# A graph layer on one core: rows that TensorE multiplies, fetched by GpSimd, ScalarE and now SyncE

## The chip, the core and the metric

The kernel runs on one core of one Trainium2 chip. The time is device time in microseconds of one execution. Before the change the median of three runs is 15399.93 us (15397.0 to 15401.84). One further execution was recorded by the hardware profiler; it took 15395.35 us, and its span from the first to the last instruction is 15393.3 us.

The names of the engines: PE is TensorE (matmul), PEld its weight load, DVE is VectorE, ACT is ScalarE, POOL is GpSimd and SP is SyncE. ACT and SP also issue DMAs; an ending q (ACTq, SPq) marks such instructions of an engine's queue.

## The reference, cut to what matters

There are 50000 nodes with 160 numbers each (64 scalars and 32 vectors of 3) and 1650000 edges: 800000 random ones in both directions, and one from each node to itself. They are sorted by destination. For each edge the row `x[src]` is fetched, combined with the edge's four numbers `e` and small weight matrices, and summed at `dst`:

```python
ss, vv = (s[src], v[src])
dot = jnp.einsum('eui,ei->eu', vv, e1)
out0 = C0 * (ss * e0 @ W1 + dot * INV3 @ W2)
...
m_agg = jax.ops.segment_sum(m, dst, num_segments=n)
h = jnp.concatenate([hs, hv.reshape(n, 3 * MUL1)], axis=1)
return x + jax.nn.relu(h)
```

After that each node's row gets its layer norm. Since everything between the fetch and the sum is linear, the kernel first sums, for every destination, the source rows weighted with each of the edge's four numbers, and applies the weights once for each node.

## The kernel before, in words

**Units, tiles, sets.** 128 edges are a unit. A unit needs the 128 rows `x[src]`, 640 bytes each, one in each partition of a tile `xg`. Six units make a group and three groups a pair (`PG = 3`; 18 units; there are 696 pairs). The change's title calls a pair a tile. Seven pairs (21 groups, 126 units) make a set (`SG`), and the edges' own data (source, destination, four numbers) are loaded a set at a time.

**Fetching rows.** `gather` (L427) fetches a unit's rows with one indirect DMA on POOL (L433), which takes the 128 row numbers from a tile `sources`. The tile `xg` has four buffers of one pair each. POOL does almost nothing else.

**Rows that ACT fetches.** One unit in every 2.5 pairs isn't gathered by POOL. `ask_alone` (L402) lets ACT fetch its rows one by one: for each of the four groups of 32 rows a register load (TENSOR_LOAD, L416) reads 32 byte addresses from the tile `where`, and then 32 DMAs of 640 bytes follow (L421), each with a register move before it. They land in `alone_scalar`, which has three buffers. `address` (L394) makes `where` for a set on DVE (L398, L399). `ask_alone` is a generator that yields after every row; the main loop takes three rows after each unit (`ALONE["scalar"]` is `(2.5, 0, 3)`: a unit every 2.5 pairs, offset 0, three rows a step) and begins a unit `LEAD` = 4 pairs ahead of the pair that uses it. PE waits for the 128 landings on a semaphore just before the unit's matmul (in `group_sums`, L465).

**Multiplying.** For each unit `spread` (L438) makes on DVE the weight tile `ha` (L445): at which of 32 nearby destinations an edge lands, times its four numbers. It does so for a whole pair, `AHEAD` = 3 pairs before its use; `ha` has `AHEAD + 1` buffers. PE multiplies `ha` by the rows (L474) and sums a group's six units in PSUM. `turn_sums` (L484) transposes the sums of the last pair on DVE (L488) and adds them into a ring of node sums (L497).

**Work beside it.** Every 7.1 pairs four blocks of nodes are finished: SP loads their rows `xt` (L741), PE multiplies the ring by the weights (L812), DVE takes the norm (L815 to L900), with a square root on ACT (`do_root`, L894), and SP writes `out` (L906). As often, SP loads the rows of a new segment of 512 nodes, `xr` in four parts, with the numbers `sa` of their edges to themselves (`ask_own`, L773 and L776), five pairs ahead, and DVE begins the segment's part of the ring with them (`set_own`). SP also loads each set's edges (`load`, L275 and L269, at the beginning of the set before it), DVE turns them (`do_cast`, `place`), and `place` also gives `sources` to POOL. Last, the edges of nodes to themselves have to be taken out of the list, so that they take no unit: 16 packs do this on DVE for 128 stretches of 790 edges each; SP reads a pack's input (L571 to L575) and stores it row by row: a register load (L698), then 16 DMAs of 18.5 KB and 0.5 KB in turn (L715), 17 such steps in a pack.

**What sets the order.** SP, PE, DVE and ACT run their instructions in the order in which the code issues them; the main loop over pairs `p` and units `j` is that order. After each unit's matmul it issues some of the work beside it (`work`, with a queue of tasks that `hand_over` fills after a pair), then some rows of `ask_alone`, then a step of the current pack as its due time wants it. An instruction that waits holds all that stands behind it on its engine.

## Time and profile before

| what | value |
|---|---|
| median of three runs | 15399.93 us |
| the profiled execution's own time | 15395.35 us |
| its span | 15393.3 us |
| mean granted TensorE clock | 0.576 |
| gathers on POOL | 12249 |
| units fetched by ACT | 267 (34176 rows) |
| rows' DMAs on SP | none |

How to read it: the page gives busy time by engine, but register loads, moves, semaphore waits and the issuing of DMAs are not counted as busy. ACT is therefore shown as 1% busy though it issues DMAs most of the time, and SP isn't in the list at all. What ACT and SP do is read from the timeline of their queues, where consecutive instructions of one kind are merged into one row with their count. A matmul in float32 appears as two records, so a unit counts double on PE.

### The profile page before, as it was taken

What the parts mean: (1) busy time and instruction counts of PE and PEld (TensorE: products, weight loads), DVE (VectorE), ACT (ScalarE), POOL (GpSimd) and SP (SyncE); (2) the same over time, 40 slices, a digit from 0 to 9 for tenths busy, and PEclk for the clock granted to TensorE, in tenths of its full rate; (3) what the DMA queues carried; (4) which work ended last, traced back from release to release, by engine and by line L of the source; (5) the groups of instructions that cost most, each with busy time, mean ns of one, the idle gap of its engine ahead of it and who ended that gap; (6) DMA issues with size and microseconds to landing.
All of it is one profiled execution on the core that took longest, in us unless ns stands there. A gap on an engine that the chain in (4) does not pass through costs nothing.

```text
span 15393.3 us, 164322 instructions
## 1 busy us (share of the span) xinstructions
PE 10745.6 (70%) x28959; PEld 6884.0 (45%) x28960; DVE 6891.3 (45%) x9468; ACT 138.6 (1%) x172; POOL 11614.3 (75%) x12263
## 2 busy tenths in 40 slices
PE   6767767676667676666766776766767676667666
PEld 3444444444444444444444444444444444444444
DVE  5534535344353544535344453544535435354333
ACT  0000000000000000000000000000000000000000
POOL 7777777777777777777777777777777777777777
PEclk5555555555555555555556555555555555555555
DMA  3333333333333333333333333333333333333332
GB/s 99 81 99 80 86 93 82 97 83 89 90 85 91 86 87 90 86 92 83 96 84 85 95 80 98 80 88 90 84 95 82 90 90 84 92 85 85 84 83 71
DMA packets 778898, 1347.79 MB, mean 88 GB/s; under 512 B 277566, under 2 KB 536537, under 8 KB 761621
## 3 DMA queue, kind: packets, MB, share of 16 engines
q0 software_dynamic: 587952, 1004.22, 27.7%
q1 hardware_dynamic: 120272, 310.14, 7.3%
q10 hardware_dynamic: 69616, 22.89, 0.8%
q14 instruction: 828, 6.77, 0.2%
q8 instruction: 230, 3.77, 0.1%
HBM read 1264.17 MB, written 72.09 MB: 87 GB/s over the span
## 4 chain that ended last, share of the span: by engine, by line
POOL 60%; issue 23%; DMA 12%; PE 4%; DVE 1%; POOLq 0%
POOL xg L433 60%; DMA xg<-in_x,sources 12%; PE ps L474 3%; PE phb L812 0%; DVE ha L445 0%; DVE xt L815 0%; DVE st L817 0%; DVE xr L791 0%; DVE ring L497 0%; DVE prow L663 0%; DVE ring L795 0%; DVE pri L658 0%; DVE sums L488 0%; DVE mv L819 0%; DVE marks L656 0%
## 5 line engine op out<-in xcount | busy, mean ns | idle before, releaser
L433 POOL DMA_INDIRECT xg<-in_x,sources x12249 | 11609.0, 948 | 3753.2 <-issue 3539.1
L474 PE MATMUL ps<-xg,ha 128*128 128x160 f32 x24498 | 9834.9, 513 | 4624.8 <-DMA xg<-in_x,sources 4521.5
L474 PEld LDWEIGHTS ps<-xg,ha 128*128 128x128 f32 x24498 | 5780.7, 293 | 8482.6 <-DMA xg<-in_x,sources 8005.4
L488 DVE STREAM_TRANSPOSE sums<-ps 128x480 f32<-128x480 f32 x696 | 474.3, 681 | 6929.9 <-PE ps L474 6909.2
L445 DVE TENSOR_TENSOR ha<-hot,pk 128x2304 f32<-128x2304 f32 x696 | 1776.0, 2552 | 23.9
L812 PE MATMUL phb<-BWk,ring 128*128 128x160 f32 (+1 forms) x3910 | 1294.8, 421 | 6.0 <-issue 5.2
L812 PEld LDWEIGHTS phb<-BWk,ring 128*128 128x128 f32 (+1 forms) x3910 | 1104.5, 325 | 7.0 <-issue 5.5
L497 DVE TENSOR_TENSOR ring<-ring,sums 128x160 f32 x2086 | 684.6, 328 | 354.2 <-issue 206.8
L815 DVE SCALAR_TENSOR_TENSOR xt<-phb,xt 128x320 f32<-128x320 f32 x196 | 96.0, 490 | 970.7 <-PE phb L812 970.6
L442 DVE TENSOR_TENSOR hot<-bank,rel 128x576 f32<-128x576 f32 x696 | 521.0, 749 | 0.1
L663 DVE COPY_PREDICATED prow<-marks,prow 128x4734 f32<-128x4734 int32 (+6 forms) x80 | 432.7, 5409 | 0.6
L795 DVE STREAM_TRANSPOSE ring<-xr 128x2560 f32<-128x2560 f32 x96 | 429.3, 4472 | 3.3
L663 DVE COPY_PREDICATED pra<-marks,pra 128x3156 f32<-128x3156 int32 (+6 forms) x80 | 294.8, 3684 | 0.0
L791 DVE TENSOR_TENSOR xr<-xr,bank 128x2560 f32<-128x2560 f32 x96 | 270.1, 2814 | 9.4 <-DMA xr<-in_x 6.1
L474 PE MATMUL ps<-alone_scalar,ha 128*128 128x160 f32 x534 | 196.5, 471 | 0.0
L474 PEld LDWEIGHTS ps<-alone_scalar,ha 128*128 128x128 f32 x534 | 160.1, 335 | 0.0
L494 DVE TENSOR_TENSOR ring<-ring 128x199 f32<-128x199 f32 (+20 forms) x485 | 150.1, 375 | 2.3
L894 ACT ACTIVATE rstd<-mv,eps_t 128x4 f32<-128x4 f32 (+1 forms) x99 | 29.4, 297 | 13513.0 <-DVE mv L819 12291.4
L900 DVE TENSOR_SCALAR xt<-xt,mv,rstd 128x160 f32<-128x160 f32 x391 | 123.2, 376 | 3.6
L751 DVE MEMSET ring<- 128x1255 f32 (+2 forms) x97 | 109.8, 1131 | 20.1 <-issue 19.9
L817 DVE BATCH_NORM_STATS2 st<-xt 128x6 f32<-128x160 f32 x391 | 108.1, 318 | 6.7
L377 DVE STREAM_TRANSPOSE pk<-raw 128x512 f32<-128x512 f32 x100 | 104.2, 1042 | 2.5 <-DMA raw<-in_attr 2.5
(342 smaller groups left out, 1661.5 us busy)
## 6 DMA issues: line engine op xcount, KB each, us to landing
alone_scalar<-in_x ACTq DMA_DIRECT2D x34176, 0.6 KB
xg<-in_x,sources POOLq DMA_INDIRECT x12249
xr<-in_x SPq DMA_DIRECT2D x380, 320.0 KB
edges<-prow SPq DMA_DIRECT2D x2030, 18.5 KB
raw<-edges SPq DMA_DIRECT2D x97, 384.0 KB
selves<-mine SPq DMA_DIRECT2D x2028, 0.5 KB
xt<-in_x SPq DMA_DIRECT2D x97, 320.0 KB
out<-xt SPq DMA_DIRECT2D x97, 320.0 KB
```

Of the source, the lines that this page charges most:

```text
L433: tc.add_to_no_dep_group(f"gathered{s % 2}", nc.gpsimd.indirect_dma_start(out=xg[:, j, :], out_offset=None, in_=x, in_offset=bass.Indirect ...
L442: nc.vector.tensor_tensor(hot[:, :n], slotsP[:, 0:W].unsqueeze(1).to_broadcast([P, n, W]), rel[:, u:u + n].unsqueeze(2).to_broadcast([P, n ...
L445: nc.vector.tensor_tensor(ha[:, :n], hot[:, :n].unsqueeze(2).to_broadcast([P, n, NK, W]), pk[:, :, u:u + n].rearrange("p k u -> p u k").un ...
L474: mm = nc.tensor.matmul(ps[:, j // G, :], ha[:, j].rearrange("p k w -> p (k w)"), xr, start=j % G == 0, stop=j % G == G - 1)
L488: nc.vector.transpose(at[:, :ng], ps[:, :ng].rearrange("p g (b f) -> p g b f", f=FB))
L494: nc.vector.tensor_tensor(ring[k][:, b, :past], ring[k][:, b, :past], ring[k - 1][:, b, S:S + past], op=ALU.add)
L497: nc.vector.tensor_tensor(here, here, at[:, i], op=ALU.add)
L663: nc.vector.copy_predicated(what[:n, a:e], mi[:, r].unsqueeze(2).to_broadcast([n, e - a, what.shape[2]]), what[:n, a + d:e + d])
L791: nc.vector.tensor_tensor(xr[:, :nq], xr[:, :nq], sumP[:, :nq].unsqueeze(2).to_broadcast([P, nq, D]), op=ALU.mult)
L795: nc.vector.transpose(ring[k][:, :, c0:c0 + nq * W].rearrange("p b (w q) -> p q b w", q=nq), xr[:, :nq].rearrange("p q (b f) -> p q b f", ...
L812: wrote("misc", nc.tensor.matmul(ph[:nb, h - h0], nodes, BWk[:, i, :], start=i == 0, stop=i == ND - 1))
L900: nc.vector.tensor_scalar(xt[:n, h], xt[:n, h], mv[:n, h, 0:1], rstd[:n, h:h + 1], op0=ALU.subtract, op1=ALU.mult)
```

## The change

SP fetches units too. `ALONE` gets `"sync": (3.0, 1, 3)`: one unit in 3 pairs, that is in 54 units, from pair 22 on; it is the last unit of its pair, and ACT's is now the one before the last. The rows of both are dealt evenly: after each unit a share of 1.03 x 128 / (every x 18) rows is added for each engine (2.44 for SP, 2.93 for ACT) and that many whole rows are issued, in place of three. Each engine has its own three buffers.

The other numbers go with it. A unit is begun 6 pairs ahead in place of 4 (`LEAD`), the segment's own rows are asked 7 pairs ahead in place of 5 (`OWN`), a set's edges are loaded in the fifth pair of the set two before it, which is 10 pairs ahead of its first use in place of 7 (`EARLY`), and `address` is issued in the second pair of a set in place of the third. The packs are due two or three pairs earlier, to match. `AHEAD` goes from 3 to 2, so `ha` has three buffers in place of four, and `place` is issued two pairs ahead of the next set.

```diff
-AHEAD = 3
+AHEAD = 2
-ALONE = {"scalar": (2.5, 0, 3)}
-LEAD = 4
+ALONE = {"sync": (3.0, 1, 3), "scalar": (2.5, 0, 3)}
+LEAD = 6
+OWN = 7
+EARLY = 4
...
+        alonep = {name: later_pools.enter_context(tc.tile_pool(name=f"alone_{name}", bufs=ALONE[name][2])) for name in ALONE}
...
         def do_cast(s):
             raws[s] = cast(raws[s])
-            address(*raws[s])
...
-            due.append(min((first - 1) * per - 1, first_of[own] // PG - 5))
+            due.append(min((first - 2) * per + EARLY - 1, first_of[own] // PG - OWN))
...
-                after_pair(p - 5, ask_own, k, bs, got)
+                after_pair(p - OWN, ask_own, k, bs, got)
...
-            if p % per == 0 and s + 1 < NSC:
-                end = reach(s + 1)
+            early = 1 if p == 0 else s + 2 if p % per == EARLY else NSC
+            if early < NSC:
+                end = reach(early)
...
-                raws[s + 1] = load(s + 1)
+                raws[early] = load(early)
+            if p % per == 1 and s + 1 < NSC and (s + 1) * SG >= NH:
+                address(*[raws[s + 1][i] for i in (0, 1, 5)])
...
-                    for _ in range(ALONE[name][2]):
-                        if name in asking and next(asking[name], 0) == 0:
+                    if name in asking:
+                        share[name] += 1.03 * P / (ALONE[name][0] * PG * G)
+                    while name in asking and share[name] >= 1:
+                        share[name] -= 1
+                        if next(asking[name], 0) == 0:
                             del asking[name]
```

On POOL the program changes in the number of gathers of a set. These rows are the start of its program before; the two `sources` tiles belong to alternate sets, and a full set is 126 gathers.

```order
L536 IOTA at 16x128
L433 DMA xg<-in_x,sources_136 128x160 x71
L433 DMA xg<-in_x,sources_137 128x160 x126
L433 DMA xg<-in_x,sources_136 128x160 x126
L433 DMA xg<-in_x,sources_137 128x160 x123
```

The same rows now:

```order
L538 IOTA at 16x128
L435 DMA xg<-in_x,sources_139 128x160 x78
L435 DMA xg<-in_x,sources_140 128x160 x126
L435 DMA xg<-in_x,sources_139 128x160 x126
L435 DMA xg<-in_x,sources_140 128x160 x121
```

From the fourth set on a set has 120 or 121 gathers in place of 123 or 124. Over the whole program the count goes from 12249 to 12029; ACT fetches 266 units in place of 267, and SP 221.

On SP these rows stand in the fourth set before, where the first units fetched row by row are asked for (`sa` and `xr` are a segment's own rows, `fd` and `raw` a set's edges):

```order
L773 DMA sa<-selves 128x1x64
L776 DMA xr<-in_x 32x2560 x4
L906 DMA out<-xt 128x640
L275 DMA fd<-edges 128x1x1
L269 DMA raw<-edges 128x2x384
L741 DMA xt<-in_x 128x640
```

And now, from the first row that SP asks for:

```order
L908 DMA out<-xt 128x640
L743 DMA xt<-in_x 128x640
L418 TENSOR_LOAD where
L423 DMA alone_sync<-in_x 1x640 x32
L418 TENSOR_LOAD where
L423 DMA alone_sync<-in_x 1x640 x11
L775 DMA sa<-selves 128x1x64
L778 DMA xr<-in_x 32x2560
L423 DMA alone_sync<-in_x 1x640 x10
L778 DMA xr<-in_x 32x2560
```

What stood together on SP now has rows between it, and a load that waits holds rows behind it. In all, SP issues 28288 rows and 884 register loads more.

More of the change, by code (lines that the diff above doesn't have):

```diff
@@ L240, in tile_gnn_resnorm @@
             tc.tile_pool(name="psM", bufs=1, space=PSUM) as psM, ExitStack() as later_pools:
-        wherep, alonep = (later_pools.enter_context(tc.tile_pool(name=name, bufs=bufs))
-                          for name, bufs in (("where", 2), ("alone", 3)))
+        wherep = later_pools.enter_context(tc.tile_pool(name="where", bufs=2))
+        alonep = {name: later_pools.enter_context(tc.tile_pool(name=f"alone_{name}", bufs=ALONE[name][2])) for name in ALONE}
         spotp, ownp = (later_pools.enter_context(tc.tile_pool(name=name, bufs=bufs))
@@ L392, in tile_gnn_resnorm, with address @@
         kept = {name: [tc.alloc_semaphore(f"own_{name}{i}") for i in range(SEMS)] for name in ALONE}
-        def address(s, at, fd, ef, af):
+        def address(s, at, ef):
             where = wherep.tile([P, NK, W], I32, name="where")
@@ L408, in ask_alone @@
             eng, kind = {"sync": (nc.sync, ET.SP), "scalar": (nc.scalar, ET.Activation)}[name]
-            to = alonep.tile([P, D], F32, name=f"alone_{name}")
+            to = alonep[name].tile([P, D], F32, name=f"alone_{name}")
             sem, uses = kept[name][asked[name] % SEMS], asked[name] // SEMS + 1
@@ L996, in tile_gnn_resnorm @@
         to_ask = {name: deque(range_of(every, at)) for name, (every, at, _) in ALONE.items()}
-        asking = {}
+        asking, share = {}, {name: 0.0 for name in ALONE}
         turning = None
         for p, (s, g, ng) in enumerate(pairs):
-            if p % per == 0 and s + 1 < NSC:
-                end = reach(s + 1)
+            early = 1 if p == 0 else s + 2 if p % per == EARLY else NSC
+            if early < NSC:
+                end = reach(early)
                 assert end <= 0 or rows_stored[0] == NR or end <= row_start(rows_stored[0])[0][0]
-                raws[s + 1] = load(s + 1)
-                if s + 2 == NSC:
-                    after_pair(p + 4, examine_all)
-                    after_pair(p + 6, read_flags)
+                raws[early] = load(early)
+            if p % per == 1 and s + 1 < NSC and (s + 1) * SG >= NH:
+                address(*[raws[s + 1][i] for i in (0, 1, 5)])
+            if p % per == 0 and s + 2 == NSC:
+                after_pair(p + 4, examine_all)
+                after_pair(p + 6, read_flags)
             if p % per == 2 and s + 1 < NSC:
```

## The prediction

> **What bounds the kernel now.** The page comes first: the engines, the groups, the chain that ended last.

> ```profile
> span 15393.3 us, 164322 instructions
> PE 10745.6 (70%) x28959; PEld 6884.0 (45%) x28960; DVE 6891.3 (45%) x9468; ACT 138.6 (1%) x172; POOL 11614.3 (75%) x12263
> POOL 60%; issue 23%; DMA 12%; PE 4%; DVE 1%; POOLq 0%
> L433 POOL DMA_INDIRECT xg<-in_x,sources x12249 | 11609.0, 948 | 3753.2 <-issue 3539.1
> L663 DVE COPY_PREDICATED prow<-marks,prow 128x4734 f32<-128x4734 int32 (+6 forms) x80 | 432.7, 5409 | 0.6
> q0 software_dynamic: 587952, 1004.22, 27.7%
> q10 hardware_dynamic: 69616, 22.89, 0.8%
> ```

> POOL's gathers are 60% of the chain, and most of the rest is "issue", the time before a gather in which it waits for nothing visible. POOL's 75% busy is thus a full engine: 948 ns of work and some 0.3 us of pause for each of 12249 gathers. The waits of POOL and three rows of its timeline (first, tenth from the last, last) confirm it.

> ```profile
> POOL xg L433 <- issue: 3539.1, 11606, 0.4
> POOL xg L433 <- PE ps L474: 154.9, 508, 0.3
> POOL xg L433 <- DMA xg<-in_x,sources: 50.8, 108, 1.8
> 6.13 1.13 POOL L433 DMA_INDIRECT xg<-in_x,sources  x1 [0.43 <-DVE center L330]
> 15354.61 0.95 POOL L433 DMA_INDIRECT xg<-in_x,sources  x1 [0.30 <-issue]
> 15367.11 0.95 POOL L433 DMA_INDIRECT xg<-in_x,sources  x1 [0.30 <-DMA xg<-in_x,sources]
> ```

> No wait for another engine is above 0.3 us, the usual pause. The last ten gathers come every 1.250 us; over all, (15367.11 - 6.13) / 12248 = 1.254 us. So a gather that is not issued is worth 1.25 us, as long as nothing else comes too late.

> ACT is the second engine to look at, since it does today what SP is to do.

> ```profile
> L421 ACTq DMA_DIRECT2D alone_scalar<-in_x x34176: 227/228/1754, 388.0 to 15100.3; - x200
> L416 ACTq TENSOR_LOAD <-where x1068: 2140/2298/4294, 385.7 to 15087.6; - x178
> 7047.19 0.30 ACT L894 ACTIVATE rstd<-mv,eps_t 128x4 f32<-128x4 f32 x1 [151.94 <-DVE mv L819]
> 7047.25 148.16 ACTq L421 DMA_DIRECT2D alone_scalar<-in_x  x364
> 7201.05 0.30 ACT L894 ACTIVATE rstd<-mv,eps_t 128x4 f32<-128x4 f32 x1 [153.56 <-DVE mv L819]
> 7355.20 150.11 ACTq L421 DMA_DIRECT2D alone_scalar<-in_x  x363
> 7509.75 145.70 ACTq L421 DMA_DIRECT2D alone_scalar<-in_x  x351
> ```

> Register loads included, a row costs ACT 148.16 / 364 = 0.407 us, a unit 52.1 us; a unit is wanted every 14712.3 / 267 = 55.1 us. In the cycle shown ACT ends its rows at 7195.41 and waits 5.6 us for DVE before the square root: it is nearly full, and not late.

> SP's own work today is one such cycle of loads (about 7 pairs), and the stores of the packs: a register load and 16 DMAs a step, 17 steps. The last rows are first and last store of a step, then the last store of that pack.

> ```profile
> 7223.61 0.36 SPq L906 DMA_DIRECT2D out<-xt  x1
> 7224.02 0.43 SPq L741 DMA_DIRECT2D xt<-in_x  x1
> 7224.49 0.58 SPq L275 DMA_DIRECT2D fd<-edges  x1
> 7225.12 0.61 SPq L269 DMA_DIRECT2D raw<-edges  x1
> 7246.43 0.54 SPq L773 DMA_DIRECT2D sa<-selves  x1
> 7253.80 1.73 SPq L776 DMA_DIRECT2D xr<-in_x  x4
> L698 SPq TENSOR_LOAD <-spots x272: 1157/1252/1925, 91.1 to 14280.1; - x136
> 7375.02 0.32 SPq L715 DMA_DIRECT2D edges<-prow  x1
> 7381.05 0.23 SPq L715 DMA_DIRECT2D selves<-mine  x1
> 7615.91 0.23 SPq L715 DMA_DIRECT2D selves<-mine  x1
> SPq L715 <- DMA edges<-prow: 365.3, 778, 3.2
> SPq L715 <- DMA selves<-mine: 208.5, 611, 1.8
> SPq L906 <- DVE xt L900: 9020.1, 95, 127.7
> ```

> A cycle's loads are 4.25 us. A step is 1.25 + 6.26 us and two gaps, 7.6 us; the waits for earlier stores, (365.3 + 208.5) / 272 = 2.1 us, bring it to 9.7 at most. I take 8.0. A pack's stores spread over 241 us. SP's long wait at L906 is idle time that rows can use.

> **The change, part by part.**

> *Gathers removed.* 220 x 1.250 to 1.254 = 275.0 to 275.9 us; I take 275.5, all of it on the path. A pair now has 18 - 1/2.5 - 1/3 = 17.27 gathers, 21.65 us in place of 17.6 x 1.254 = 22.07.

> *Rows on SP: do they fit?* They are asked from pair 16 on, and the last unit is used in pair 682: of 15125 us, 16 and 13 pairs of 18 x 1.254 us fall away, and 14470 remain. No trace shows rows on SP, so ACT's are the nearest. Lower bound: 0.407 us a row, 52.1 a unit. Upper: two sequencers issuing at once may slow each other. While SP stored a pack, ACT's rows took 150.11 / 363 = 0.4135 and 145.70 / 351 = 0.4151 us, 7 to 8 ns more, at 272 / 241 = 1.13 SP DMAs a microsecond. (One register load more or less in such a stretch is 2.3 / 360 us, 6 ns a row, so this is known to a factor of two at best.) ACT will issue 128 / 54.1 = 2.37, 2.1 times as many, so by proportion 14 to 17 ns: 0.421 to 0.424. It can't well be below nothing, since neither sequencer does anything for the other. I take 0.421, 53.9 us a unit, because the loaded stage is the nearer row. Then 221 x 53.9 = 11912, 15 packs (the first is stored before) x 17 x 8.0 = 2040, and 95 cycles x 4.25 = 404: 14356 of 14470 us, 99.2%. With the lower bounds (52.1 and 7.6) it is 95.8%, with the upper ones (54.3 and 9.7) 102.8%.

> Of the register loads the rows say 2.30 us for 32 values and 1.25 for 16. [...]

> *ACT, in less time.* A unit is now wanted every 2.5 x 21.65 = 54.1 us. SP will issue 128 / 65.0 = 1.97 rows a microsecond, 1.74 times the rate of the loaded stage, plus its stores a quarter of the time: 14 ns on average, 0.421 us a row, 53.9 a unit; 266 units and 94 square roots at 0.30 are 14365 us of 14490. It fits by 1%.

> *Leads.* A unit's rows are dealt over 128 / 2.44 = 52 units, 2.9 pairs, so they are asked 4.0 pairs, 87 us, before use. Landing takes what a gather's takes:

> ```profile
> 7004.40 2.57 DMA xg<-in_x,sources
> ```

> That leaves 84 us. In a store stage SP has 17 x 8.0 + 241 x 53.9 / 65.0 + 241 x 4.25 / 152 = 343 us of work in 241, so it ends 102 late; off the stages it has 14% spare and wins back about 100 in the 700 us to the next. PE would then wait some 18 us for rows at a stage's end. Four `xg` buffers let POOL run three pairs, 65 us, ahead of a late PE; `place` gives it new `sources` 2.8 pairs, 61 us, ahead. So POOL first waits where SP is 145 us late. Own rows (4 pairs after the last part's request), sets of edges (4 pairs to `address`) and `xt` (3.5 pairs, 76 us) stand behind the same rows on SP: DVE may wait some 25 us for `xt`, and POOL still doesn't. For ACT the same margin is 4.5 pairs less the landing, 94 us, and 60 more: some 150 us in all.

> *At nothing.* `ha` two pairs ahead in place of three: 43 us cover DVE's longest instruction, 5.4 us (L663); without the cover PE waits, not POOL, up to those 61 us. `address` one pair earlier moves half a microsecond on DVE; it can make SP and ACT wait for `where` only where DVE is late for a set's edges, and these are now asked 3 pairs sooner. PE gets 221 more semaphore waits, hidden by its 30% of idle time. The DMA engines get 28288 rows, 0.7% more by q10's 0.8% for ACT's.

> Sum: the profiled 15395.35 lies 4.6 us under the median of 15399.93 and the removed work is the same in both, so the median becomes 15399.9 - 275.5 = 15124.4; rounded, 15125.

> **The rivals.**

> *Slower: two row streams slow each other.* Place: each row's issue on ACT and SP. If they share one path, a row could cost far more than 14 ns extra, since the store stage had only 1.13 DMAs a microsecond against it, in bursts. ACT uses up its 14490 us, its 150 us of margin and the whole gain at 14915, that is at 0.437 us a row, 30 ns above 0.407; that is the point. At 35 ns its work is 266 x 128 x 0.442 + 28 = 15077 us, and the time 15125 + (15077 - 14640) = 15560. For it: both sequencers are at 99%, with no room for error. Against: twice the extra measured in the loaded stage would still be gone only in part. Chance 0.10.

> *Store stages spill over.* Steps at 9.7 us and rows at 0.424 make 102.8%, 404 us too much; less the 145 us that SP may be late before POOL waits, up to 260 is lost: 15385. A middle case, 102%, is 289 too much, loses 144 and comes to about 15270. For it: the lag of 102 us is won back only just. Against: the waits of 2.1 us come where stores follow one another, and rows now lie between steps. Chance 0.18, of it 0.05 so near the end that the time is within 0.2%.

> *The gathers' pace is not POOL's.* If the 16 DMA engines set the 1.25 us, rows moved to another queue take the same engines' time and nothing is won: 15400. Against it, gathers under different traffic (the first column behind the window is its length, then busy time and count, clock, DMA share, GB/s):

> ```profile
> 400.00:2000.00 1600.00, 1210.25 (x1279) 0.57 0.36 87
> 15150.00:15390.00 240.00, 165.03 (x175) 0.58 0.30 70
> ```

> 946 and 943 ns, at 0.36 and 0.30 of the DMA engines, of which gathers have 27.7%: the price follows POOL's work. Chance 0.02. [...]

> That the change doesn't do what it says is excluded by the program's rows: 12029 gathers, 221 units on SP.

> **How the numbers follow.** The forecast, 15125, has 0.70. Faster by over 0.2% (30 us, about what a measurement of this kernel can tell from no change) are the forecast and the spill up to 15369: 0.70 + 0.13 = 0.83. Within 0.2%: 0.05 + 0.02 = 0.07. Slower: 0.10. The forecast's own range is 15095 (all that the mean pace has over 1.250 us is won as well, 12029 x 0.004 = 48, of which I allow 30) to 15200. The whole range goes on to the spill's end, 15390; what lies above is the first rival and half of the cases without change, some 0.13, and little lies below.

> **What would show it.** Right: some 12029 gathers still every 1.25 us; no POOL wait for PE above the 0.3 us pause; ACT's and SP's rows at 0.42 us; PE waiting up to 20 us at the ends of store stages. Wrong: rows at 0.43 us or more on either; POOL waiting microseconds for PE or DVE; ACT never again waiting for DVE before a square root; gathers slower than 948 ns.

## The result and the profile after

| | before | changed kernel |
|---|---|---|
| median | 15400.88 us (15397.0 to 15401.84, 4 runs) | 16068.88 us (16059.6 to 16097.72, 4 runs) |
| ratio to before, 95% interval | | 1.0438 [1.0421, 1.0454] |
| profiled execution, span | 15393.3 us | 16057.9 us |
| gathers on POOL | 12249 | 12029 |

Faster was forecast, and the kernel is 4.4% slower. These are the page's lines of the changed kernel: the span, the queues, the chain and two groups.

```profile
span 16057.9 us, 221715 instructions
q0 software_dynamic: 577392, 986.19, 27.8%
q1 hardware_dynamic: 176848, 328.36, 7.4%
q10 hardware_dynamic: 69360, 22.81, 0.9%
PE 0%; DMA 0%; DVE 0%; POOL 0%; issue 0%
L435 POOL DMA_INDIRECT xg<-in_x,sources x12029 | 11398.8, 948 | 4627.2 <-issue 3150.1
L476 PE MATMUL ps<-alone_sync,ha 128*128 128x160 f32 x442 | 171.2, 490 | 1002.2 <-PEq L475 1002.2
```

The chain is of no use here: its shares are all 0%. The group of the gathers says more. There are 220 fewer and each still takes 948 ns, but POOL's idle time before them has risen from 3753.2 to 4627.2 us. A second group is new: PE waits 1002.2 us at L475 for rows that SP fetched. Two stories offer themselves, and POOL's waits in the changed kernel tell which of them holds POOL (total us, times, longest us):

```profile
POOL xg L435 <- issue: 3150.1, 10119, 3.6
POOL xg L435 <- DMA xg<-in_x,sources: 1390.5, 1708, 3.6
POOL xg L435 <- PE ps L476: 72.9, 180, 4.2
```

For PE it waits hardly at all (72.9 us, of which 180 x 0.3 are the usual pauses). What has grown is a gather's wait for another gather's landing, from 50.8 us in 108 waits to 1390.5 in 1708. Taken from the start times of all gathers, what each comes later than 1.251 us after the one before adds up to 53 us in the kernel before and to 990 us here. That is the result: 990 - 53 = 937, less the 275.5 saved, is 662 us, and the span has grown by 664.6.

The loss isn't spread evenly. Three stretches of the changed kernel (length, POOL's busy time and gathers, clock, DMA share, GB/s), of which the middle one is a store stage of SP:

```profile
7175.00:7550.00 375.00, 237.90 (x252) 0.56 0.35 76
7650.00:8050.00 400.00, 300.71 (x317) 0.58 0.36 86
8150.00:8340.00 190.00, 119.00 (x127) 0.57 0.35 76
```

In the store stage, where SP has both rows and stores to issue, a gather comes every 400 / 317 = 1.26 us, as before. Off the stages, where SP has time for its rows, one comes only every 190 / 127 = 1.50 us. So POOL stands where SP is early, not where it is late. The DMA engines' share is the same 0.35 to 0.36 in all three, no higher than the 0.36 of the kernel before. These are POOL's waits in the store stage and then in the last stretch:

```profile
POOL xg L435 <- issue: 96.9, 307, 3.6
POOL xg L435 <- DMA xg<-in_x,sources: 1.2, 4, 0.3
```

```profile
POOL xg L435 <- DMA xg<-in_x,sources: 48.6, 58, 1.8
POOL xg L435 <- issue: 22.1, 67, 1.9
```

And this is POOL gather by gather in that stretch (start, length, the pause before it and what ended it):

```profile
8201.49 0.94 POOL L435 DMA_INDIRECT xg<-in_x,sources  x1 [1.75 <-DMA xg<-in_x,sources]
8202.97 0.94 POOL L435 DMA_INDIRECT xg<-in_x,sources  x1 [0.54 <-DMA xg<-in_x,sources]
8204.98 0.94 POOL L435 DMA_INDIRECT xg<-in_x,sources  x1 [1.07 <-DMA xg<-in_x,sources]
8206.23 0.95 POOL L435 DMA_INDIRECT xg<-in_x,sources  x1 [0.30 <-issue]
```

Which gather's landing is it? Each gather's record names its semaphore. There are eight, 142 to 149, used in turn, and each gather adds to its own in sixteen steps. So a gather has to wait until the one eight before it has landed, and eight are issued in 8 x 1.25 = 10 us. Put beside each other from the trace (us from the span's start):

```
gather    pause   eight before:  issued   15th step  16th step
8201.49    1.75                 8188.25    8190.81    8201.23
8202.97    0.54                 8189.56    8192.25    8202.71
8204.98    1.07                 8190.81    8194.76    8204.72
8206.23    0.30                 8192.06    8194.94    8205.54
```

Each of the three held gathers starts 0.26 us after the sixteenth step of the gather eight before. Of 1254 pauses above 0.5 us in the whole trace, 1081 end within 0.5 us of that step. And it is only the sixteenth that is late: in these four rows fifteen steps are done 2.6 to 4.0 us after issue, the last one 13.0 to 13.9 us. Over the whole last stretch the medians are 2.6 and 11.2 us, in the store stage 2.6 and 6.8. Over all gathers whose sixteen steps could be read:

```
                 15th step: median, 95%     16th step: median, 90%, 95%     16th after more than 10 us
before               2.57    5.93               2.64    6.22    7.07              0.4%
changed kernel       2.60    4.40               7.62   11.60   12.18             27.8%
```

If the sixteen steps come from sixteen DMA engines, fifteen of them are as quick as before, and one is late. (The steps alone don't show that it is the same one for every gather.) What could fill one alone? The queues' packet counts suggest an answer. SP's queue q1 went from 120272 to 176848, which is 56576 = 2 x 28288: two packets for each of SP's rows, one of 640 bytes and one of 4 bytes. A gather has 587952 / 12249 = 48, of which 16 are of 4 bytes, as many as its steps. The account from here on takes it that each packet of 4 bytes stands for one engine: a row then has a single engine, a gather all sixteen, and all rows are taken to have the same one. That is the author's estimate from these counts and from the one late step; no trace shows it, since packets carry no engine number.

The rows' own landings fit too. For each row its semaphore has one entry some 0.1 us after the issue and one at the landing. Where all of a unit's entries are in the trace (about one unit in eight here), SP's rows land 10.2 us after issue in the median and ACT's 9.3, about as late as the gathers' last step off the store stages. ACT's rows in the kernel before land after 1.4 us. So rows of both queues and one step of the gathers are held up together, while the gathers' other steps aren't.

Off the store stages both sequencers issue rows one after another (start, length and count of merged issues, ACT's and SP's):

```profile
8185.77 151.85 ACTq L423 DMA_DIRECT2D alone_scalar<-in_x  x354
8272.53 52.30 SPq L423 DMA_DIRECT2D alone_sync<-in_x  x128
```

That is 2.33 + 2.45 = 4.8 rows a microsecond, by this account on one engine, which also has its sixteenth of every gather. The whole last stretch has packets of 431 rows of SP and 441 of ACT: (431 + 441) / 190 = 4.6 a microsecond. In the store stage there are 523 and 943: (523 + 943) / 400 = 3.7.

### The profile page after: what moved, and what is told of

The parts are those of the page before. It is cut to its first block, busy times and chain, and to the rows that moved or that the text cites. A ratio compares the mean times of both kernels' runs of the same rounds, so it can differ in the third digit from the quotient of the medians.

```text
span 16057.9 us, 221715 instructions
## 1 busy us (share of the span) xinstructions
PE 9917.3 (62%) x28959; PEld 6747.6 (42%) x28960; DVE 6880.0 (43%) x9464; ACT 141.5 (1%) x172; POOL 11404.2 (71%) x12043
## 3 DMA queue, kind: packets, MB, share of 16 engines
q0 software_dynamic: 577392, 986.19, 27.8%
q1 hardware_dynamic: 176848, 328.36, 7.4%
## 5 line engine op out<-in xcount | busy, mean ns | idle before, releaser
L435 POOL DMA_INDIRECT xg<-in_x,sources x12029 | 11398.8, 948 | 4627.2 <-issue 3150.1
L476 PE MATMUL ps<-xg,ha 128*128 128x160 f32 x24058 | 8928.9, 492 | 4871.3 <-DMA xg<-in_x,sources 4672.4
L476 PEld LDWEIGHTS ps<-xg,ha 128*128 128x128 f32 x24058 | 5587.3, 288 | 8013.4 <-DMA xg<-in_x,sources 7493.7
L499 DVE TENSOR_TENSOR ring<-ring,sums 128x160 f32 x2086 | 684.8, 328 | 339.6 <-issue 208.5
L476 PE MATMUL ps<-alone_sync,ha 128*128 128x160 f32 x442 | 171.2, 490 | 1002.2 <-PEq L475 1002.2
L476 PEld LDWEIGHTS ps<-alone_sync,ha 128*128 128x128 f32 x442 | 126.7, 328 | 1021.5 <-PEq L475 1021.5
```

Source lines behind the costliest of these rows:

```text
L435: tc.add_to_no_dep_group(f"gathered{s % 2}", nc.gpsimd.indirect_dma_start(out=xg[:, j, :], out_offset=None, in_=x, in_offset=bass.Indirect ...
L476: mm = nc.tensor.matmul(ps[:, j // G, :], ha[:, j].rearrange("p k w -> p (k w)"), xr, start=j % G == 0, stop=j % G == G - 1)
L499: nc.vector.tensor_tensor(here, here, at[:, i], op=ALU.add)
```

## The experiments

**The same rows in fewer transfers.** Each DMA of SP fetches 16 neighbouring rows into 16 partitions. 15 of 16 rows are then other rows than those asked for; their bytes, the gathers and the matmuls stay. (Addresses are clipped at N - 16, and the count that PE waits for becomes 8 DMAs a unit.)

```diff
...
+                        if name == "sync" and k % 16:
+                            yield
+                            continue
+                        m = 16 if name == "sync" else 1
-                        d = eng.dma_start(to[e:e + 1, :]..., xbytes[ds(v[k], 4 * D)]...(o=1))
+                        d = eng.dma_start(to[e:e + m, :]..., xbytes[ds(v[k], m * 4 * D)]...(o=m))
```

> The kernel in which each of SP's DMAs fetches 16 rows that follow one another (the first is the row asked for, the other fifteen are other rows than those asked for), once more, since the whole run before it was some 60% slow for every kernel, the one before the change too. Theory A (one of the sixteen DMA engines takes every one-row DMA and is filled by ACT's and SP's together): such a DMA is dealt over all sixteen, the sixteenth landing is as before the change, 15125 to 15170 us. Theory B (SP asks too late): SP has much less to issue, 15125 to 15170 too. A third theory, that the sum of the traffic is too much: the same bytes, so near 16050.

Measured: 15122.08 us (15119.82 to 15124.34, 2 runs), 0.9815 [0.9786, 0.9843] of before. The page's span and queue, the gathers, and POOL's wait for landings:

```profile
span 15122.3 us, 168675 instructions
...
q1 hardware_dynamic: 176848, 328.36, 7.9%
...
L439 POOL DMA_INDIRECT xg<-in_x,sources x12029 | 11408.0, 948 | 3682.4 <-issue 3487.7
```

```profile
POOL xg L439 <- DMA xg<-in_x,sources: 42.9, 102, 2.4
```

SP's queue has the very packets of the changed kernel, 176848 of them and 328.36 MB (56576 / 1768 = 32 for each DMA of 16 rows in place of 2 for one of a row, in A's terms sixteen engines in place of one), and there is no surplus. C is out. The sixteenth step is back at a median of 2.65 us, and ACT's rows land after 1.3 us again. The other edits of the change (requests further ahead, three `ha` buffers) cost nothing, since they are all in this kernel. But SP also issues 1768 DMAs in place of 28288 and is never late, so A and B are both still in. So is a rival of A, that the number of DMAs issued counts, whichever engines carry them. No undisturbed run separates it from A; against it stand the fifteen steps of each gather that come as early as ever.

**SP less late, with as many rows.** SP loads 32 addresses once in a unit and uses them for all four groups, so that 96 of 128 rows are other rows than asked for. Three register loads a unit, 7 us of SP's time, go; the one-row DMAs stay.

```diff
+                    if name == "scalar" or i == 0:
-                    _, v = nc.values_load_multi_w_load_instructions(
+                        _, v = nc.values_load_multi_w_load_instructions(
```

> The change, but SP loads addresses once for a unit and fetches the same 32 rows four times (96 of the unit's 128 rows are left out and 32 come four times); once more, on a chip at its usual speed. SP saves three register loads, about 7 us of 54 a unit, and issues as many one-row DMAs. Theory A (one of the sixteen DMA engines takes every one-row DMA): that engine has the same load, a gather's sixteenth landing stays near 10 us, POOL's excess over 1.251 us a gather stays at 800 to 1000 us, and the time is 15950 to 16100, though PE hardly waits for SP's rows. Theory B (SP asks too late, PE waits, POOL behind it): SP has 12% of room, PE's waits go, and the time is 15125 to 15200.

Measured: 16234.22 us (16230.84 to 16245.08, 4 runs), 1.0544 [1.0526, 1.0561] of before, above what A expected. POOL's wait for landings, and PE's for SP's rows:

```profile
POOL xg L436 <- DMA xg<-in_x,sources: 1596.2, 1749, 5.6
```

```profile
PE ps L477 <- PEq L476: 238.2, 23, 27.8
```

PE waits a quarter of what it did (238.2 for 1002.2 us), and the kernel is 165 us slower. B as the cause of the loss falls here. POOL's wait for landings has grown, and A offers a reason: between pauses (gaps under 3 us) SP's rows come every 0.363 us in place of 0.415. That this accounts for all of the 165 us isn't shown.

**SP's rows without ACT's.**

```diff
-ALONE = {"sync": (3.0, 1, 3), "scalar": (2.5, 0, 3)}
+ALONE = {"sync": (3.0, 1, 3)}
```

> ACT fetches no rows, SP its 221 units with all its other work; once more, on a chip at its usual speed. Theory A: with about 1.97 one-row DMAs a microsecond in place of 4.3 the sixteenth landing of a gather stays under 7 us, POOL's excess is under 120 us, and the time is that of 12295 gathers at 1.254 us and 38 us around them, 15455. Theory B: SP's own work is the same, so PE's waits for its rows stay near 1000 us and the time near 16000 to 16100.

Measured: 15459.42 us (15456.78 to 15461.53, 5 runs), 1.0039 [1.0025, 1.0053]. The gathers and POOL's wait for landings:

```profile
L435 POOL DMA_INDIRECT xg<-in_x,sources x12295 | 11653.0, 948 | 3769.7 <-issue 3566.3
```

```profile
POOL xg L435 <- DMA xg<-in_x,sources: 54.0, 113, 2.0
```

12295 x 1.254 + 38 = 15455.9, so the surplus is 3.5 us. SP's rows do no harm by themselves, and they land after 1.4 us; the two engines' rows together do the harm.

**A smaller share for SP.**

```diff
-ALONE = {"sync": (3.0, 1, 3), "scalar": (2.5, 0, 3)}
+ALONE = {"sync": (4.5, 1, 3), "scalar": (2.5, 0, 3)}
```

> SP fetches one unit in about 63 instead of one in 54 of the gathers' share, so 12102 gathers are left on POOL (73 more than in the changed kernel). Theory A (one of the 16 DMA engines takes every one-row transfer, and where ACT and SP together fill it a gather's sixteenth landing comes later than the 10 us in which eight gathers are issued): POOL's excess lies somewhere between the 53 us of the kernel before and the 990 us of the changed one, and falls by far more than the share of rows does; 12102 x 1.254 + 38 = 15214 us if the queue does not stand at all, up to 15360 us with 150 us of waits. Theory B (SP asks too late for PE): SP's slack grows by some 10 us per unit, and the time is 15214 us with no stage left over. Third (total traffic): in proportion to the rows, about 16000 us.

Measured: 15485.54 us (15473.44 to 15494.72, 5 runs), 1.0055 [1.0041, 1.0068], 125 us more than A's upper bound. POOL's wait for landings, and the two longest of PE's, among which L475 is no more:

```profile
POOL xg L435 <- DMA xg<-in_x,sources: 460.5, 685, 3.0
```

```profile
PE ps L476 <- DMA xg<-in_x,sources: 4747.3, 7374, 6.3
PE ps L476 <- DVE sums L490: 49.9, 62, 0.9
```

PE no longer waits for SP's rows, and 271.6 us of surplus are left: B gives none of them. C's 16000 is 514 us too high. In A's terms the waits begin gradually, and the mean of 3.7 rows a microsecond, on which the forecast for this share rested, was the wrong measure, since the rate varies within a run. Cut into stretches of 50 us, this trace has 218 of 330 us of late gathers in stretches with more than 4 rows a microsecond; the changed kernel has 935 of 985. The runs side by side:

```
                         one-row DMAs   gathers   median us   surplus us   16th step: median, 95%   over 10 us
before                        34176      12249    15400.88        2.6          2.64    7.07            0.4%
SP's rows alone               28288      12295    15459.42        3.5          2.65    6.02            0.4%
SP 16 rows a DMA              34048      12029    15122.08       -0.3          2.65    6.56            0.3%
SP 1 unit in 4.5 pairs        52992      12102    15485.54      271.6          6.01   10.80            8.3%
changed kernel                62336      12029    16068.88      946.5          7.62   12.18           27.8%
SP with one load a unit       62336      12029    16234.22     1111.8          7.85   13.69           24.6%
```

**Runs on other chips.** Fourteen runs went to other chips, five by their numbers, on which every kernel took some 60% longer, the kernel before too (24526 to 24816 us), so their times decide nothing here. ACT's rows in the run without SP's come there every 286.41 / 390 = 0.73 us in this stretch:

```profile
7227.62 286.41 ACTq L423 DMA_DIRECT2D alone_scalar<-in_x  x390
```

Four kernels ran nowhere else, and what they were to tell stays open. The first leaves SP's rows out (`ALONE = {"scalar": (2.5, 0, 3)}`), the second has `"sync": (6.0, 1, 3)`, and the third fetches 40 bytes of each of SP's rows in place of 640 and leaves the rest of the row zero:

```diff
+                        b = 40 if name == "sync" else 4 * D
-                        d = eng.dma_start(to[e:e + 1, :]..., xbytes[ds(v[k], 4 * D)]...)
+                        d = eng.dma_start(to[e:e + 1, :b // 4]..., xbytes[ds(v[k], b)]...)
```

> The changed kernel without SP's rows: the sets of edges ten ahead, rows asked six tiles ahead, ACT's share as before, 12250 gathers. Theory A: the other edits cost nothing, so the time is that of the kernel before, 15400 us (within 30). If the earlier requests themselves cost something (more rows and edges under way, other buffers), it is above 15430 us.

> SP fetches one unit in about 81 of the gathers' share; 12139 gathers are left on POOL. With SP at 4.5 the time was 15485 us, which is 271 us above 12102 x 1.254 + 38 = 15214, and with SP at 3.0 it was 16069 us, 944 us above its 15125. Theory A: the surplus falls further with the rows per us on the one DMA engine, to 0 to 130 us: 12139 x 1.254 + 38 = 15260 us, up to 15390, below the kernel before. Total traffic in proportion to the rows: half of 944, about 15700 us.

> SP issues as many one-row DMAs as in the changed kernel, of 40 bytes instead of 640. If the one DMA engine is filled by the number of transfers, POOL's waits stay: near 16050 us. If it is filled by their bytes, SP's rows weigh a sixteenth, POOL's excess falls to near the 53 us of the kernel before, and the time is 12029 x 1.254 + 38 = 15125 us, up to 15300. Theory B (SP asks too late for PE) expects no change, 16050 us, since the issues are the same.

Measured, against the kernel before on the same chip each: 25808.3 us, 1.0505 [1.0490, 1.0519], without SP's rows; 25837.33, 1.0508 [1.0482, 1.0535], with SP at 6.0; 25976.39, 1.0577 [1.0559, 1.0595], with 40 bytes. The first of them, without any row on SP, loses nearly as much as the others; POOL waits there for PE, 7265.5 us, and not for landings. So these times tell nothing about the theories, and why the earlier requests cost 5% there was not looked into. Their traces don't help either: all sixteen steps can be read for fewer than 100 of some 12000 gathers.

The earlier runs of these three kernels, and one run or two of each of the others, went to such chips too. What had been expected of them, and their ratios there:

SP's rows without ACT's: 25300.99 us, 1.0184 [1.0145, 1.0223].

> ACT fetches no rows any more, SP its 221 units with all its other work. Theory A (one of the sixteen DMA engines takes every one-row DMA; ACT's and SP's rows together fill it, a gather's share there lands last, and POOL waits for the gather eight before): with about 1.97 rows a microsecond in place of 4.3 the sixteenth landing of a gather stays under 7 us, POOL's excess over 1.251 us a gather goes from 990 us to under 120, and the time is that of 12295 gathers at 1.254 us and 38 us around them, 15455. Theory B (SP asks too late because its own work fills it; PE waits for its rows, and POOL is held up behind PE): SP's work is the same, so PE's waits for the rows' semaphore stay near 1000 us and the time near 16000 to 16100.

Without SP's rows: 26065.88 us, 1.0487, and 25883.62, 1.0515.

> All of the change but SP's rows: leads of 6, 7 and 10 pairs, rows dealt by shares, two pairs of weights ahead. Both theories: 12250 gathers, 15400 within 30 us. If the shorter lead of the weights or the moved loads cost anything, it is slower by that.

> All of the change but SP's rows (leads of 6, 7 and 10 pairs, rows dealt by shares, weights two pairs ahead), once more on a chip at its usual speed. Theory A: the number of one-row DMAs is that of before, 12250 gathers, 15400 within 30 us. If these edits cost anything by themselves, it is slower by that.

One load a unit: 26065.14 us, 1.0505.

> The change, but SP loads addresses once for a unit and fetches the same 32 rows four times (96 of the unit's 128 rows are left out and 32 come four times). SP saves three register loads, about 7 us of 54 a unit, and issues as many one-row DMAs. Theory A: the DMA engine has the same load, POOL's excess stays at 800 to 1000 us, and the time is 15950 to 16100 though PE hardly waits for SP's rows. Theory B: SP has 12% of room, PE's waits go, and the time is 15125 to 15200.

16 rows a DMA: 25697.39 us, 1.0356.

> The change, but each of SP's DMAs fetches 16 rows that follow one another in x, into 16 partitions (the first of them is the row asked for, the other fifteen are other rows than those asked for). The bytes and rows are the same, in 8 DMAs a unit. Theory A: a DMA of 16 rows is dealt over all sixteen DMA engines, the one engine is left with ACT's rows, the sixteenth landing is as before the change, and the time is 15125 to 15170. Theory B: SP has much less to issue, so 15125 to 15170 too. A third theory, that the sum of the traffic is too much for the DMA engines or the memory: the same bytes, so near 16050.

SP at 4.5: 25898.11 us, 1.0548, and 25922.82, 1.0549.

> The change with SP fetching one unit in 4.5 pairs in place of 3 (148 units, 12102 gathers). Theory A (one DMA engine takes every one-row DMA, and is full where SP and ACT issue 4.7 of them a microsecond): on average 2.37 + 1.31 = 3.7 a microsecond, below that; the sixteenth landing stays mostly under 10 us, POOL's excess falls from 990 us to under 200, and the time is 12102 x 1.254 + 38 = 15214 to 15360. If the number of rows in all were no matter and only SP's being in order, 15214.

> SP fetches one unit in 4.5 pairs in place of 3 (148 units, 12102 gathers), once more on a chip at its usual speed. Theory A (one DMA engine takes every one-row DMA, and is full where SP and ACT issue 4.7 of them a microsecond): on average 2.37 + 1.31 = 3.7 a microsecond, below that; the sixteenth landing stays mostly under 10 us, POOL's excess falls from 990 us to under 200, and the time is 12102 x 1.254 + 38 = 15214 to 15360. If the number of rows in all were no matter, 15214.

SP at 6.0: 25794.24 us, 1.0507.

> The same with one unit in 6 pairs (111 units, 12139 gathers), 2.37 + 0.98 = 3.35 one-row DMAs a microsecond. Theory A: no full DMA engine, POOL's excess near that of before (53 us), 12139 x 1.254 + 38 = 15260, within 30 us. It is faster than both kernels.

40 bytes of each row: 25960.65 us, 1.0561, and 25945.39, 1.0546.

> The change, but SP fetches only the first 40 of each row's 640 bytes (the other 600 are left out, and DVE clears the tile first). As many one-row DMAs from SP, a sixteenth of their bytes. Theory A with a cost for each DMA: the engine is as full as before, 15900 to 16100. Theory A with a cost for the bytes: the engine has what it has from ACT alone, 15125 to 15250.

> The change, but SP fetches only the first 40 of each row's 640 bytes (the other 600 are left out, and DVE clears the tile first), once more on a chip at its usual speed. As many one-row DMAs from SP, a sixteenth of their bytes. Theory A with a cost for each DMA: the engine is as full as before, 15900 to 16100. Theory A with a cost for the bytes: the engine has what it has from ACT alone, 15125 to 15250.

None of these met its expectation, all of which were worked out for chips like the first.

The fourth is SP at 4.5 with each row in four pieces. They are kept from being one by a gap of 4 bytes in the tile:

```diff
-            to = alonep[name].tile([P, D], F32, name=f"alone_{name}")
+            parts = 4 if name == "sync" else 1
+            to = alonep[name].tile([P, parts, D // parts + parts // 4], F32, name=f"alone_{name}")[:, :, :D // parts]
```

> As the run with SP at 4.5 (15485 us), but SP's rows lie in the tile as four pieces of 160 bytes with a gap of 4 bytes between them, so that each one-row DMA is four transfers and can go to four DMA engines instead of one; the same bytes arrive, and PE reads around the gaps. Theory A: the fullest engine gets a quarter of each of SP's rows instead of the whole, the sixteenth landing falls back to the others', the waits of 334 us go, and the time is 12102 x 1.254 + 38 = 15214 us, up to 15290; the issue may cost SP more per row, for which there is slack at this share. If the number of transfers on the fullest engine counts and not their bytes, it stays at 15485 us. Theory B and the total traffic see no reason for a gain: 15485 us or more, since SP's issues are as many and the transfers four times as many.

Measured: 28976.52 us, 1.1814 [1.1795, 1.1832], where whole rows at that share had 1.0549. Its time decides nothing about landings either, but its trace does tell something. First SP's queue on its page, and then on that of a run with whole rows at the same share, also on one of these chips:

```profile
q1 hardware_dynamic: 271824, 322.57, 4.0%
```

```profile
q1 hardware_dynamic: 158160, 322.34, 4.4%
```

And SP's issues (shortest, median and longest ns), in the same order:

```profile
L424 SPq DMA_DIRECT2D alone_sync<-in_x x18944: 2/577/1729, 618.5 to 28652.2; - x200
```

```profile
L423 SPq DMA_DIRECT2D alone_sync<-in_x x18944: 2/228/1649, 616.1 to 25560.3; - x200
```

(271824 - 158160) / 18944 = 6 packets more a row: four pieces in place of one, and four of 4 bytes. If each of these four comes from an engine of its own, such a row had four engines, but the trace doesn't number them. And the issue has a median of 577 ns in place of 228, and ACT's whole rows have 273 in place of 228, so SP could fetch far fewer rows in this way. It is no remedy as it stands.

## Why the prediction was wrong

**The step that failed** stands under *At nothing*: "The DMA engines get 28288 rows, 0.7% more by q10's 0.8% for ACT's." The sum over sixteen engines is right (q10 is at 0.9%, the DMA share unchanged), but it is the wrong quantity. If rows of ACT and SP have one engine between them, as theory A has it, the 0.8% of sixteen were 12.8% of that one. By their recorded times the rows' packets of 640 bytes add up to 10.4% of the span in the kernel before and to 22.9% in the changed one; on one engine they stand beside the 27.8% that gathers take of the sixteen on average. The DMAs were costed by bandwidth, and what decided was the latest of sixteen landings against the 10 us that eight gathers take. The third rival came nearest: it asked whether DMA engines set the gathers' pace, and its test used gathers under different traffic (946 and 943 ns). But that is the length of the instruction on POOL, 948 ns in the changed kernel too; the time is lost between instructions, and in the kernel before POOL waited for landings only 50.8 us. Among the signs of being wrong a wait of POOL for another gather's landing is missing.

**Gathers removed: right.** With the disturbance gone the price holds: 15122.08 us measured with 16 rows a DMA, for 15124.4 forecast, though there SP has far less to issue.

**A row's issue: right.** 0.421 us was forecast for both engines. ACT has 151.85 / 354 = 0.429 us, and SP 52.30 / 128 = 0.409 in the lines shown; over the whole run, gaps above 3 us left out, ACT has 0.419 and SP 0.415. The rival in which two streams slow each other at issue needed 0.437 and more; its time, 15560, was on the right side for another reason, which is luck.

**SP's sum: too small.** Stores wait longer between rows than taken, and SP's idle time has gone; these are its own waits in the changed kernel:

```profile
SPq L717 <- DMA edges<-prow: 877.2, 703, 7.7
SPq L908 <- DVE xt L902: 312.5, 7, 99.2
SPq L717 <- DMA selves<-mine: 123.7, 437, 1.6
```

The stores wait 877.2 + 123.7 = 1000.9 us, 427 more than before; the step of 8.0 us had room for 0.4 x 272 = 110. Of the 9020.1 us of idle time at the wait for `xt` 312.5 are left. So SP, forecast at 99.2%, is full or over it.

**Leads: partly.** PE's waits were to be some 18 us at a stage's end. They average 19.3 us (1002.2 / 52), the longest is 48.5, and there are more of them than the 15 stage ends. POOL doesn't stand behind them, as predicted, but here it had 946 us of waits of its own, so this doesn't show that four `xg` buffers would have been enough at 15125 us. What whole rows on SP would cost a kernel without late landings was not measured.

**What stays open.** That all one-row DMAs have one and the same engine wasn't seen directly, since no packet carries an engine's number; the late steps and the late rows of both queues speak for it. Whether the number of transfers or their bytes make the engine late was not settled either. The packets' recorded times don't add up to a full engine (22.9 and 27.8%, and some 11% for all the rest if that is spread evenly, over the whole span), so the trace doesn't show what makes it late. At SP 6.0 the surplus may be small enough for a gain over the kernel before (12139 gathers, 15260 us without any), but no undisturbed run shows it, and of the kernels that fetch the rows asked for none beat the one before.

## What to carry to other kernels

Before small DMAs are moved to another queue, ask into how many packets each of them goes: a one-row DMA of SP or ACT had a single packet of data here, where a gather had 32, and the mean share of the DMA engines, 0.35 to 0.36 with held gathers and without, didn't tell that anything was late. A gather's semaphore was used again here only after the last of its sixteen steps, at a median of 7.62 us where the fifteenth came at 2.60; so count the one-row transfers a microsecond of all queues together, stretch by stretch and not as the mean of a run, and hold the last of a gather's steps, not the median landing, against the time until its semaphore is used again (10 us here). An experiment that keeps the bytes and changes only the number of DMAs (16 rows in one) tells such a cause from bandwidth in one run.

## What the runs showed of the hardware

- One-row DMAs of 640 bytes from two queues made gathers land late while the DMA share showed nothing of it: in a stretch with 3.7 a microsecond POOL wasn't held, in one with 4.6 the sixteenth step came 11.2 us after issue in the median where the other fifteen took 2.6, with a share of 0.35 to 0.36 in both.
- The rows were late with the gathers: in the changed kernel SP's landed after 10.2 us in the median and ACT's after 9.3, where those of either queue alone took 1.4.
- A sequencer with less to do made the kernel slower: without three register loads a unit of SP the time rose by 165 us.
- A row in four pieces of 160 bytes took SP a median of 577 ns to issue in place of 228 (both on the slower chips), sixteen neighbouring rows in one DMA 342 ns:

```profile
L427 SPq DMA_DIRECT2D alone_sync<-in_x x1768: 315/342/1390, 384.8 to 14667.9; - x197
```
